# Thresholds from group maxima in the second attention step, with a list of rows done later

## The chip, the cores and the metric

The kernel runs on one core of a Trainium2 chip. The metric is the device time of one execution in microseconds (us); lower is better. Before the change the median of 3 runs was 5419.04 us (5407.9 to 5441.06). The engines are PE (TensorE, the matrix products; PEld are its weight loads), DVE (VectorE), ACT (ScalarE), POOL (GpSimd, which also issues DMAs) and SP (which issues DMAs).

## The reference, cut to what matters

Four graph layers over N = 4096 nodes with D = 256 features. Layers 0, 2 and 3 are products of the adjacency matrix with the features. Layer 1 makes two steps of attention in which each row keeps the largest probabilities until their sum reaches 0.9 of the whole ("top-p"):

```python
def _top_p_attention(X, W1, W2, W3):
    q = X @ W1.T @ W2.T
    k = X @ W3.T
    logits = q @ k.T / TAU
    probs = jax.nn.softmax(logits, axis=-1)
    idx = jnp.argsort(-probs, axis=-1)
    sp = jnp.take_along_axis(probs, idx, axis=-1)
    cs = jnp.cumsum(sp, axis=-1)
    keep_sorted = cs - sp < TOP_P
    ...
    A = probs * mask
    return A / jnp.maximum(A.sum(-1, keepdims=True), 1e-12)
...
for n in range(STEPS):
    A = _top_p_attention(Xa, W1, W2, W3)
    Xf = R @ Xf
    Xa = A @ Xa
    Z = Z + Xf @ U1[n].T + Xa @ U2[n].T
h = X + Z
```

Here n is step 0 and step 1, and R is the adjacency matrix with its diagonal raised by one, each row divided by its sum. The sort is stable, so among equal probabilities the node with the lower number comes first: where the threshold falls inside a set of equal ones, the first of them are kept and the last dropped. h is then normalized over its features, scaled and shifted, added to the layer's input and normalized once more.

## The kernel before, in words

The rows are worked in 32 tiles of 128 rows (P). For a tile the logits against all 4096 nodes form a 128 x 4096 array.

`run_step(n)` goes through i from -2 to 31 and holds three tiles at a time: nxt (tile i + 2), for which PE makes the logits, in 8 chunks of 512; cd (tile i + 1), for which DVE and ACT find the threshold; and st (tile i), for which `pieces` (L455) transposes the masked e on PE (`turn`, L468), copies it out on ACT (L470) and multiplies it with the features (acc_a, L487), beside the adjacency product (acc_r, L483; its blocks come over SP's queue, 256 KB each). `pieces` has 8 pieces, g = 0 to 7, and after piece g it issues what `ops` lists for g. `mix` (L504) then multiplies both results with U1 and U2 (z_ps, L515), and in step 0 makes the keys of step 1 (k_ps, L157). Within an engine the instructions run in a fixed order, which the framework sets when the kernel is built; it keeps nearly to the order of the program, and moves instructions forward when it reckons that they are ready.

Step 0 finds the threshold so: `peak_groups` (L287) takes the eight largest logits of each of 16 groups of 256 columns (MAX8, L277), 128 candidates; their maximum m goes to ACT, which makes e = exp(l - m) with its sum z (`exp_rows`, L279 to L285); `pick(cd, 6)` (L338) takes the 48 largest candidates in six rounds of MAX8 and match-replace, their running sum (L361), and the entry at which the sum reaches thr = 0.9 z (L366). A row is bad if the 48 don't reach so far or if a group's eighth candidate is not below the threshold. A one-column product on PE (bad_ps, L394) sums bad over the rows; `settle` (L404) reads the sum into a register of DVE (L411), branches on it, and then masks e in four quarters of 1024 columns, with their sums (L444). A tie at the threshold is told by v > 0, a row that isn't covered by v > P - 1.

Step 1 finds it in another way, whose cost lies on DVE: `peak` (L296) reduces the whole row for m; `bracket` (L301) makes five probes, each a pass over the 4096 columns that sums what is not below a trial value (L325), masks the array once more (L334) and takes MAX8 of 16 groups of it; `pick(cd, 8)` follows with 64 candidates; and `settle` always tells ties apart, with three passes: equality (L400), a running sum over the columns (L401), a difference (L402).

`bit_by_bit` (L416) is the way of last resort for a tile: 30 passes over the 4096 columns, each of which settles one bit of the threshold. It stands inside a branch.

The last layernorms of step 1 (`after`) run on DVE, with a power function on POOL (L147) in each. Layers 2 and 3 follow; layer 2 loads the result x2 in chunks (x2c, L626).

The thresholds' small arrays are [128, 1], the logits l and e are separate arrays with two buffers each.

Of the kernel before, what the change touches and what calls it, by code (L numbers as in the profile page):

```python
# [20 lines left out]
P = 128  # L21
D = 256
# [10 lines left out]
PROBES = 5  # L33
AIM = 0.65
# [5 lines left out]
def gnn_stack(ctx, tc, x, adjt, adjn, w0, b0, w1t, w2t, w3t, u1t, u2t, ln_g, ln_b, w2, b2, w3, b3, out):  # L40

# [37 lines left out]
    x2_d = dram.tile([N, D], F32, name="x2_d")  # L79
    x3_d = dram.tile([N, D], F32, name="x3_d")  # L80
    xa_d = dram.tile([N, D], F32, name="xa_d")
    h_d = dram.tile([N, D], F32, name="h_d")
# [150 lines left out]
    with tc.tile_pool(name="l1", bufs=1) as l1, tc.tile_pool(name="l1w", bufs=2) as l1w:  # L233
        g_sb = load_bcast(l1, ln_g, "g_sb")
        lb_sb = load_bcast(l1, ln_b, "lb_sb")
        cur = {}

# [6 lines left out]
        def query(n, i):  # L244

            lo, hi = DA * n, DA * (n + 1)
            xt = transposed(cur["xa"][:, i, :])
# [17 lines left out]
        def new_logits():  # L265
            return l1w.tile([P, N], F32, tag="l", name="l")

        def small(tag, w=1, dt=F32):
            return work.tile([P, w], dt, tag=tag, name=tag)
# [9 lines left out]
        def exp_rows(st):  # L279

            st["e"] = l1w.tile([P, N], F32, tag="e", name="e")
            st["z"] = z = small("z")
            nc.scalar.activation(st["e"], st["l"], AF.Exp, bias=st["m"], scale=1.0, accum_out=z)
            st["thr"] = small("thr")
            nc.vector.tensor_scalar(st["thr"], z, TOP_P, None, op0=ALU.mult)  # L285

        def peak_groups(st):  # L287

            st["cand"] = cand = small("cand", 8 * ngr)
            groups(st["l"], cand)  # L290
            st["m"] = m = small("m")
            nc.vector.tensor_reduce(m, cand, axis=AX.X, op=ALU.max)
            nc.vector.tensor_scalar(m, m, -1.0, None, op0=ALU.mult)
            st["base"] = None

        def peak(st):  # L296
            st["m"] = m = small("m")
            nc.vector.tensor_reduce(m, st["l"], axis=AX.X, op=ALU.max)
            nc.vector.tensor_scalar(m, m, -1.0, None, op0=ALU.mult)

        def bracket(st):  # L301


            e, thr = st["e"], st["thr"]
# [33 lines left out]
        def pick(st, rounds):  # L338

            cand, thr, base = st["cand"], st["thr"], st["base"]
            W = 8 * rounds
            g8 = small("g8")
            nc.vector.tensor_reduce(g8, cand.rearrange("p (g k) -> p g k", k=8)[:, :, 7], axis=AX.X, op=ALU.max)
            top = small("top", W)
# [6 lines left out]
            if base is None:  # L353
                nc.vector.memset(cs[:, 0:1], 0.0)
                te = small("te", W)
# [6 lines left out]
            last, part = small("last", W), small("part", W)  # L362
            nc.vector.tensor_scalar(part, cs[:, :W], thr, None, op0=ALU.is_lt)
            nc.vector.scalar_tensor_tensor(last, cs[:, 1:], thr, part, op0=ALU.is_ge, op1=ALU.mult)
            st["t"] = t = small("t_thr")
            nc.vector.scalar_tensor_tensor(part, last, 1.0, top, op0=ALU.mult, op1=ALU.mult, accum_out=t)  # L366
            bad = small("bad")
            nc.vector.tensor_tensor(bad, g8, top[:, W - 1 : W], op=ALU.max)
            nc.vector.tensor_tensor(bad, bad, t, op=ALU.is_ge)
            if base is None:  # L370
                nxt = small("nxt")
                nc.vector.scalar_tensor_tensor(part[:, 1:], last[:, : W - 1], 1.0, top[:, 1:], op0=ALU.mult, op1=ALU.mult,
                                               accum_out=nxt)
                nc.vector.tensor_tensor(nxt, nxt, t, op=ALU.is_ge)
                nc.vector.scalar_tensor_tensor(bad, bad, float(P), nxt, op0=ALU.mult, op1=ALU.add)
            else:
                nc.vector.tensor_scalar(bad, bad, float(P), None, op0=ALU.mult)  # L377

            def room():

                te_thr, r = small("t_e"), small("room")
                nc.vector.scalar_tensor_tensor(part, last, 1.0, te, op0=ALU.mult, op1=ALU.mult, accum_out=te_thr)
                nc.vector.scalar_tensor_tensor(part, te, te_thr, te, op0=ALU.is_gt, op1=ALU.mult, accum_out=r)
                nc.vector.tensor_add(r, r, cs[:, 0:1])
                nc.vector.tensor_sub(r, thr, r)
                tp = small("tp")
                nc.vector.tensor_scalar(tp, te_thr, 1e-30, None, op0=ALU.max)
                nc.vector.reciprocal(tp, tp)
                nc.vector.tensor_mul(r, r, tp)
                return te_thr, r  # L390

            st["room"] = room
            pb = ps_mm.tile([P, D], F32, tag="mm", name="bad_ps")
            nc.tensor.matmul(pb[:1, :1], bad, ones_col, start=True, stop=True)  # L394
            st["bad"] = pb

        def tell_apart(s, e, t, room):

            nc.vector.tensor_scalar(room, room, 1.0, TINY, op0=ALU.add, op1=ALU.mult)
            nc.vector.tensor_scalar(s, e, t, -TINY, op0=ALU.is_equal, op1=ALU.mult)  # L400
            nc.vector.tensor_tensor_scan(s, s, s, room, op0=ALU.add, op1=ALU.max)  # L401
            nc.vector.scalar_tensor_tensor(s, e, t, s, op0=ALU.subtract, op1=ALU.add)  # L402

        def settle(st):  # L404

            e, thr = st["e"], st["thr"]
            ties = st["base"] is not None
            nb = work.tile([1, 1], I32, tag="nbad", name="nbad")  # L410
            nc.vector.tensor_copy(nb, st["bad"][:1, :1])  # L411
            v = nc.vector.value_load(nb[0:1, 0:1])
            s = l1.tile([P, N], F32, tag="s", name="s")
            h, fl = small("mass"), small("flip", 1, I32)

            def bit_by_bit(t, room):  # L416
                ti = t.bitcast(I32)
                nc.vector.memset(ti, 1 << (ALL_BITS - 1))
                for b in range(ALL_BITS - 1, -1, -1):
                    nc.vector.scalar_tensor_tensor(s, e, t, e, op0=ALU.is_ge, op1=ALU.mult, accum_out=h)  # L420
                    nc.vector.tensor_scalar(fl, h, thr, float(1 << b), op0=ALU.is_lt, op1=ALU.mult)
                    nc.vector.scalar_tensor_tensor(ti, fl, (1 << b) >> 1, ti, op0=ALU.bitwise_or, op1=ALU.bitwise_xor)
                nc.vector.scalar_tensor_tensor(s, e, t, e, op0=ALU.is_gt, op1=ALU.mult, accum_out=h)
                nc.vector.tensor_sub(room, thr, h)
                nc.vector.reciprocal(h, t)
                nc.vector.tensor_mul(room, room, h)

            if ties:
                t, room = st["room"]()
                with tc.If(v > P - 1):  # L430
                    bit_by_bit(t, room)
                tell_apart(s, e, t, room)
            else:
                with tc.If(v > 0):
                    t, room = st["room"]()
                    with tc.If(v > P - 1):
                        bit_by_bit(t, room)
                    tell_apart(s, e, t, room)
                    nc.vector.scalar_tensor_tensor(e, s, 0.0, e, op0=ALU.is_ge, op1=ALU.mult)
                    nc.vector.memset(st["t"], -3e38)  # L440
            kq = small("kq", NQ)
            for c in range(NQ):
                q = slice(c * QW, (c + 1) * QW)
                nc.vector.scalar_tensor_tensor(e[:, q], (s if ties else st["l"])[:, q], 0.0 if ties else st["t"], e[:, q],  # L444
# [79 lines left out]
        def after(n, i, st):  # L524
# [8 lines left out]
            def s2():  # L533
                st["ln"] = ln_stats(st["h"])
# [189 lines left out]
```

## Time and profile before

| what | us |
|---|---|
| median of 3 runs | 5419.04 (5407.9 to 5441.06) |
| the profiled execution, its own time | 5451.28 |
| its span, first to last instruction | 5449.1 |
| busy PE / DVE / ACT / POOL in the span | 4525.2 / 3220.7 / 1143.6 / 518.0 |
| step 0: first logits to last product of acc_r | 718 to 2264 |
| step 1: first logits to last settle | 2284 to 4749 |
| layer 2's first product | 4783.5 |
| mean granted TensorE clock | 0.859 |

How to read it: the span is cut into 40 equal slices, and each digit is the busy share of an engine in tenths. A group line gives line, engine, operation, output<-input, shapes and count, then busy us and mean ns of one, then the engine's idle time just before these instructions and what ended it. A timeline line gives the start, the length, the instruction and, in brackets, the idle time before it. A matmul of 32-bit floats shows as two instructions.

### The profile page before, as it was taken

The page shows a single profiled execution, that of the slowest core. Times are in us where ns is not written, and L with a number is a line of the kernel's source. Part 1 is how long each engine was busy: PE and PEld are TensorE (multiplying, and loading weights), DVE is VectorE, ACT ScalarE, POOL GpSimd, SP SyncE. Part 2 cuts the span into 40 slices and gives each one's busy share as a digit, 9 for nine tenths or more (in the row PEclk, how much of TensorE's full clock was granted, in tenths as well). Part 3 has the DMA queues.
Part 4 walks back from the last instruction along what each step waited for, and adds up shares of the span by engine and source line. Part 5 has one row for each costly group of instructions (what it writes and reads, how often), then busy time and mean ns, then how long its engine had stood idle before and what let it go on. Part 6 is the DMA issues. An engine that isn't in the chain of part 4 may idle for free. (4 is left out here: it accounts for less than half of the span.)

```text
span 5449.1 us, 54173 instructions
## 1 busy us (share of the span) xinstructions
PE 4525.2 (83%) x19520; PEld 3347.0 (61%) x19520; DVE 3220.7 (59%) x7924; ACT 1143.6 (21%) x1969; POOL 518.0 (10%) x966
## 2 busy tenths in 40 slices
PE   9999999999999899946766777666766767489999
PEld 7888866666666666735544555445544555467776
DVE  1111143333333433199999999999999999833322
ACT  1000033333333323212211222121221212011100
POOL 4444300000000000000000000000000000022222
PEclk8998799999999999867777777777777777799999
DMA  8777621111111111201101110111101111077787
GB/s 225 220 213 206 176 62 50 51 50 49 50 51 49 44 50 49 87 22 37 30 27 36 37 37 24 33 36 37 37 21 35 37 37 30 21 226 225 228 247 223
DMA packets 246758, 464.20 MB, mean 85 GB/s; under 512 B 26643, under 2 KB 82582, under 8 KB 246422
## 3 DMA queue, kind: packets, MB, share of 16 engines
q0 software_dynamic: 110592, 268.48, 17.2%
q1 hardware_dynamic: 128192, 184.60, 11.2%
q10 hardware_dynamic: 7638, 7.10, 0.4%
q8 instruction: 154, 2.52, 0.2%
q14 instruction: 182, 1.49, 0.1%
HBM read 434.92 MB, written 25.17 MB: 84 GB/s over the span
## 5 line engine op out<-in xcount | busy, mean ns | idle before, releaser
L262 PE MATMUL lg<-kT,qT 64*128 64x512 f32 x1024 | 732.6, 852 | 10.4 <-ACT qT L256 10.4
L325 DVE SCALAR_TENSOR_TENSOR junk<-e,pr 128x4096 f32<-128x4096 f32 x160 | 716.4, 4477 | 3.5
L277 DVE MAX8 cand<-l 128x8 f32<-128x256 f32 x512 | 194.5, 418 | 727.5 <-ACT l L263 727.0
L483 PE MATMUL acc_r<-x,adjq 128*128 128x256 f32 x2048 | 502.6, 386 | 59.7 <-ACT xa_new L495 57.7
L468 PE MATMUL at_ps<-ident,e 128*128 128x128 f32 x2048 | 346.3, 300 | 243.3 <-DVE e L444 243.3
L487 PE MATMUL acc_a<-xa,at 128*128 128x256 f32 x2048 | 530.8, 406 | 0.0
L468 PEld LDWEIGHTS at_ps<-ident,e 128*128 128x128 f32 x2048 | 259.5, 153 | 434.9 <-issue 417.5
L263 ACT COPY l<-lg 128x512 f32<-128x512 f32 x512 | 299.5, 585 | 1046.8 <-PE lg L262 1046.2
L487 PE MATMUL acc_a<-x,at 128*128 128x256 f32 x2048 | 488.4, 381 | 0.0
L147 POOL TENSOR_TENSOR rstd<-ve,mhalf 128x1 f32<-128x1 f32 x160 | 89.2, 558 | 4062.9 <-DVE ve L145 3847.6
L394 PE MATMUL bad_ps<-ones_col,bad 128*1 128x1 f32 x128 | 12.1, 164 | 537.3 <-DVE bad L377 537.3
L483 PE MATMUL acc_r<-xf_next,adjq 128*128 128x256 f32 x2048 | 452.7, 381 | 0.1
L483 PEld LDWEIGHTS acc_r<-x,adjq 128*128 128x128 f32 x2048 | 367.3, 191 | 135.4 <-ACT xa_new L495 65.0
L262 PEld LDWEIGHTS lg<-kT,qT 64*128 64x128 f32 x1024 | 236.2, 253 | 333.3 <-issue 200.4
L470 ACT COPY at<-at_ps 128x512 f32<-128x512 f32 x512 | 299.9, 586 | 664.7 <-PE at_ps L468 655.4
L487 PEld LDWEIGHTS acc_a<-xa,at 128*128 128x128 f32 x2048 | 400.9, 205 | 60.5 <-ACT at L470 8.8
L487 PEld LDWEIGHTS acc_a<-x,at 128*128 128x128 f32 x2048 | 387.6, 190 | 74.4 <-issue 22.7
L483 PEld LDWEIGHTS acc_r<-xf_next,adjq 128*128 128x128 f32 x2048 | 388.5, 191 | 54.9 <-issue 2.8
L123 PE MATMUL acc<-x0h,adjt 128*128 128x512 f32 x1024 | 345.9, 460 | 9.0 <-DMA adjt<-in_adjt 7.1
L394 PEld LDWEIGHTS bad_ps<-ones_col,bad 128*1 128x1 f32 x128 | 5.5, 81 | 561.2 <-DVE bad L377 550.2
L107 POOL DMA_DIRECT2D adjt<-in_adjt x512 | 279.3, 545 | 509.5 <-PE acc L123 400.2
L401 DVE TENSOR_TENSOR_SCAN s<-s,room 128x4096 f32<-128x4096 f32 x33 | 288.8, 8751 | 1.2
(184 smaller groups left out, 6230.1 us busy)
## 6 DMA issues: line engine op xcount, KB each, us to landing
adjq<-in_adjt SPq DMA_DIRECT2D x512, 256.0 KB, 2.8
adjt<-in_adjt POOLq DMA_DIRECT2D x256, 512.0 KB, 5.1
adjt<-in_adjt POOLq DMA_DIRECT2D x256, 256.0 KB, 4.3
adjn<-in_adjn POOLq DMA_DIRECT2D x256, 256.0 KB, 4.1
x_d<-x SPq DMA_DIRECT2D x64, 128.0 KB, 3.8
x<-in_x ACTq DMA_DIRECT2D x4, 1024.0 KB, 10.2
x1r<-x_d SPq DMA_DIRECT2D x32, 128.0 KB, 2.0
xa_d<-xa_new SPq DMA_DIRECT2D x32, 128.0 KB, 1.7
```

What stands on the lines that cost most here:

```text
L107: (nc.gpsimd if dt is F32R else nc.sync).dma_start(t, src[it, :, c * jp : (c + 1) * jp, :])
L123: nc.tensor.matmul(acc, a[:, j, :], halves(jt), start=(jt == 0), stop=(jt == NT - 1))
L147: nc.gpsimd.tensor_tensor(r, ve, mhalf, op=ALU.pow)
L262: nc.tensor.matmul(pl[:, :LC], qT, kT[DA * n : DA * (n + 1), s], start=True, stop=True)
L263: nc.scalar.copy(l[:, s], pl[:, :LC])
L277: nc.vector.max(dst[:, 8 * g : 8 * g + 8], src[:, g * GW : (g + 1) * GW])
L325: nc.vector.scalar_tensor_tensor(junk, e, pr[:, 0:1].bitcast(F32), e, op0=ALU.is_ge, op1=ALU.mult, accum_out=mass[id(pr)])
L401: nc.vector.tensor_tensor_scan(s, s, s, room, op0=ALU.add, op1=ALU.max)
L468: nc.tensor.transpose(ps[:, j, :], e[:, (g * G + j) * P : (g * G + j + 1) * P], ident)
L470: nc.scalar.copy(ats[g][:, :G, :], ps[:, :G, :])
L483: nc.tensor.matmul(acc_r[:, :D], adjs[g][:, j, :], cur["xf"][:, jt, :], start=(jt == 0), stop=False)
L487: nc.tensor.matmul(acc_a[:, :D], ats[g][:, j, :], cur["xa"][:, jt, :], start=(jt == 0), stop=(jt == NT - 1))
```

## The change

Step 1 now uses the way of step 0 for its 32 tiles, with eight rounds. Rows that this doesn't settle are listed in memory (their numbers, by a scatter from POOL), up to LATER * P = 512 of them; after the 32 tiles four more tiles are run, whose rows are gathered by that list and which use the bracket. A tile whose unsettled rows would not fit into the list runs `bit_by_bit` in place. The masks of both steps no longer tell ties apart with passes: pick counts `left`, how many entries equal to the threshold have to be dropped, and one match-replace over the row (with eight pad columns of -1) sets the first `left` of them to 0; the host reverses the nodes, so that the first in the array are the last in the reference. A row with left above PAD = 8 counts as bad. In step 0 and in the four tiles, any bad row sends the whole tile through `bit_by_bit`. e is computed in place of l, in three buffers.

In the diff, cut to its core, "..." marks what is left out.

```diff
+LATER = 4
+PAD = 8
...
+    x2_d = dram.tile([N + LATER * P, D], F32, name="x2_d")
...
+    xf_d = dram.tile([N, D], F32, name="xf_d")
+    list_d = dram.tile([(LATER + 1) * P, 1], I32, name="list_d")
...
         def new_logits():
-            return l1w.tile([P, N], F32, tag="l", name="l")
+            l = l1w.tile([P, N + PAD], F32, tag="e", name="e", bufs=3)
+            nc.vector.memset(l[:, N:], -1.0)
+            return l
...
         def exp_rows(st):
-            st["e"] = l1w.tile([P, N], F32, tag="e", name="e")
+            e = st["e"][:, :N]
             st["z"] = z = small("z")
-            nc.scalar.activation(st["e"], st["l"], AF.Exp, bias=st["m"], scale=1.0, accum_out=z)
+            nc.scalar.activation(e, e, AF.Exp, bias=st["m"], scale=1.0, accum_out=z)
...
-            last, part = small("last", W), small("part", W)
-            nc.vector.tensor_scalar(part, cs[:, :W], thr, None, op0=ALU.is_lt)
-            nc.vector.scalar_tensor_tensor(last, cs[:, 1:], thr, part, op0=ALU.is_ge, op1=ALU.mult)
+            under, part = small("under", W), small("part", W)
+            count = small("count")
+            nc.vector.tensor_scalar(under, cs[:, :W], thr, 0.0, op0=ALU.is_lt, op1=ALU.add, accum_out=count)
+            nc.vector.scalar_tensor_tensor(part, cs[:, 1:], thr, under, op0=ALU.is_ge, op1=ALU.mult)
             st["t"] = t = small("t_thr")
-            nc.vector.scalar_tensor_tensor(part, last, 1.0, top, op0=ALU.mult, op1=ALU.mult, accum_out=t)
-            bad = small("bad")
-            nc.vector.tensor_tensor(bad, g8, top[:, W - 1 : W], op=ALU.max)
+            nc.vector.scalar_tensor_tensor(part, part, 1.0, te[:, :W], op0=ALU.mult, op1=ALU.mult, accum_out=t)
+            st["left"] = left = small("left")
+            nc.vector.tensor_scalar(part, te[:, :W], t, 0.0, op0=ALU.is_ge, op1=ALU.add, accum_out=left)
+            nc.vector.tensor_sub(left, left, count)
+            st["bad"] = bad = small("bad")
+            nc.vector.tensor_tensor(bad, te[:, W - 1 : W], te[:, W:], op=ALU.max)
             nc.vector.tensor_tensor(bad, bad, t, op=ALU.is_ge)
...
+            nc.vector.scalar_tensor_tensor(bad, left, float(PAD), bad, op0=ALU.is_gt, op1=ALU.max)
+
+        def flag(st):
+            pb = ps_mm.tile([P, D], F32, tag="mm", name="bad_ps")
+            if st.get("later") is None:
+                nc.tensor.matmul(pb[:1, 0:1], st["bad"], ones_col, start=True, stop=True)
             else:
...
+                nc.tensor.matmul(pb[:, 0:1], ones_sq, st["bad"], start=True, stop=True)
+                nc.tensor.matmul(pb[:, 1:2], before, st["bad"], start=True, stop=True)
+            st["bad_ps"] = pb
+
+        def bit_by_bit(st, s):
+            e, thr, t = st["e"][:, :N], st["thr"], st["t"]
+            h, fl, room = small("mass"), small("flip", 1, I32), small("room")
+            ti = t.bitcast(I32)
+            nc.vector.memset(ti, 1 << (ALL_BITS - 1))
+            for b in range(ALL_BITS - 1, -1, -1):
+                nc.vector.scalar_tensor_tensor(s, e, t, e, op0=ALU.is_ge, op1=ALU.mult, accum_out=h)
+                nc.vector.tensor_scalar(fl, h, thr, float(1 << b), op0=ALU.is_lt, op1=ALU.mult)
+                nc.vector.scalar_tensor_tensor(ti, fl, (1 << b) >> 1, ti, op0=ALU.bitwise_or, op1=ALU.bitwise_xor)
+            nc.vector.scalar_tensor_tensor(s, e, t, e, op0=ALU.is_gt, op1=ALU.mult, accum_out=h)
+            nc.vector.tensor_sub(room, h, thr)
+            nc.vector.reciprocal(h, t)
+            nc.vector.tensor_mul(room, room, h)
+            nc.vector.tensor_scalar(s, e, t, 0.0, op0=ALU.is_equal, op1=ALU.add, accum_out=h)
+            nc.vector.tensor_add(room, room, h)
+            nc.vector.tensor_scalar(room, room, -TINY, None, op0=ALU.mult)
+            nc.vector.tensor_scalar(s, s, TINY, None, op0=ALU.mult)
+            nc.vector.tensor_tensor_scan(s, s, ones_col.to_broadcast([P, N]), room, op0=ALU.add, op1=ALU.min)
             nc.vector.scalar_tensor_tensor(s, e, t, s, op0=ALU.subtract, op1=ALU.add)
+            nc.vector.scalar_tensor_tensor(e, s, 0.0, e, op0=ALU.is_gt, op1=ALU.mult)
+            nc.vector.memset(t, 1e-37)
+            nc.vector.memset(st["left"], 0.0)

         def settle(st):
...
+            if later is None:
+                nc.vector.tensor_copy(nb, pb[:1, :1])
+            else:
+                sofar = small("sofar")
+                nc.vector.tensor_add(sofar, later["base"], pb[:, 0:1])
+                nc.vector.tensor_scalar(nb, sofar[:1, :1], float(LATER * P), None, op0=ALU.is_gt)
+                slot = small("slot")
+                nc.vector.tensor_add(slot, later["base"], pb[:, 1:2])
             v = nc.vector.value_load(nb[0:1, 0:1])
             s = l1.tile([P, N], F32, tag="s", name="s")
...
+            with tc.If(v > 0):
+                bit_by_bit(st, s)
+                if later is not None:
+                    nc.vector.memset(st["bad"], 0.0)
+                    nc.vector.tensor_copy(sofar, later["base"])
+            if later is not None:
+                it = later["tile"]
+                at = small("at", 1, I32)
+                nc.vector.tensor_sub(slot, slot, spare)
+                nc.vector.scalar_tensor_tensor(at, slot, st["bad"], spare, op0=ALU.mult, op1=ALU.add)
+                later["base"] = sofar
+                nc.gpsimd.indirect_dma_start(
+                    out=list_d, out_offset=bass.IndirectOffsetOnAxis(ap=at[:, 0:1], axis=0),
+                    in_=ids[:, it : it + 1], in_offset=None)
+            go, no, eight = small("go", PAD), small("no", PAD), small("eight", PAD)
+            nc.vector.tensor_scalar(go, count8, left, None, op0=ALU.is_lt)
+            nc.vector.tensor_scalar(no, go, -1.0, None, op0=ALU.add)
+            nc.vector.scalar_tensor_tensor(eight, go, t, no, op0=ALU.mult, op1=ALU.add)
+            nc.vector.match_replace(e, eight, e, 0.0)
             kq = small("kq", NQ)
             for c in range(NQ):
                 q = slice(c * QW, (c + 1) * QW)
-                nc.vector.scalar_tensor_tensor(e[:, q], (s if ties else st["l"])[:, q], 0.0 if ties else st["t"], e[:, q],
-                                               op0=ALU.is_ge, op1=ALU.mult, accum_out=kq[:, c : c + 1])
+                nc.vector.scalar_tensor_tensor(e[:, q], e[:, q], t, e[:, q], op0=ALU.is_ge, op1=ALU.mult,
+                                               accum_out=kq[:, c : c + 1])
...
+        def gathered(src, st, tag):
+            t = work.tile([P, D], F32, tag=tag, name=tag)
+            nc.gpsimd.indirect_dma_start(
+                out=t, out_offset=None, in_=src, in_offset=bass.IndirectOffsetOnAxis(ap=st["from"][:, 0:1], axis=0))
+            return t
...
+        def put_off(k):
+            st = {"tile": None}
+            st["to"] = to = small("to", 1, I32, LATER)
+            nc.sync.dma_start(to, list_d[k * P : (k + 1) * P, :])
+            st["from"] = fr = small("from", 1, I32, LATER)
+            nc.vector.tensor_scalar(fr, to, float(N - 1), None, op0=ALU.min)
+            st["q"] = query(n, gathered(xa_d, st, "xg"))
+            st["e"] = new_logits()
+            return st
...
+            end = NT + 1 + LATER if last_step else NT
+            for i in range(-2, end):
...
+                elif NT < i + 2 < end:
+                    nxt = put_off(i + 2 - NT - 1)
...
+                if cd is not None and cd["tile"] is not None:
+                    if later is not None:
+                        later["tile"] = cd["tile"]
+                    peak_groups(cd)
+                    at(1, exp_rows, cd)
+                    at(2, pick, cd, 8 if last_step else 6)
+                    at(4, flag, cd)
+                    at(5, settle, cd)
+                    pieces(n, st, nxt, ops)
                 else:
                     if cd is not None:
                         bracket(cd)
...
+                    pieces(n, st, nxt, ops)
                     if cd is not None:
                         pick(cd, 8)
+                        flag(cd)
+                if nxt is not None and nxt["tile"] is None:
+                    peak(nxt)
+                    exp_rows(nxt)
+                if cd is not None and cd["tile"] is None:
+                    settle(cd)
...
+    x = np.asarray(x)[::-1]
+    adj = np.asarray(adj)[::-1, ::-1]
...
+    return r.results[0]["out"][::-1]
```

Before the change `pick` and `settle` stood at pieces 3 and 4 in step 0. In the four added tiles `pieces` makes no acc_r: xf is stored to xf_d by the 32 tiles of step 1 and gathered, as are h_d, x1_d and xa_d, and the result is scattered to x2_d.

## The prediction

> **What bounds the kernel now.** I read the slices first, then the windows (busy time of each engine in a stretch), the waits of step 1, the groups by cost and shape, and the timelines of one tile.
>
> ```profile
> PE   9999999999999899946766777666766767489999
> DVE  1111143333333433199999999999999999833322
> PEclk8998799999999999867777777777777777799999
> ```
> Each digit is one slice of 136 us. In slices 5 to 16 (step 0) TensorE is full and VectorE works a third of the time. In slices 17 to 34 (step 1) it is the other way round.
>
> ```profile
> 1400.00:1800.00 400.00, 385.22 (x1707) 273.84 (x1707) 143.81 (x525) 135.59 (x229) 0.00 (x0) 1.00 0.16 50
> 3000.00:4000.00 1000.00, 698.95 (x2678) 503.72 (x2678) 959.46 (x2045) 204.68 (x330) 14.24 (x26) 0.74 0.11 33
> ```
> Columns: window, length, then busy us of PE, PEld, DVE, ACT, POOL, the granted clock, DMA. Step 0 has PE at 96%; step 1 has DVE at 96% and PE at a clock of 0.74, because it waits:
>
> ```profile
> PE bad_ps L394 <- DVE bad L377: 475.9, 30, 16.5
> PE at_ps L468 <- DVE e L444: 214.5, 30, 21.1
> ```
> (us in total, times, longest.) The DVE work of a step-1 tile is full-width passes:
>
> ```profile
> L325 DVE SCALAR_TENSOR_TENSOR junk<-e,pr 128x4096 f32<-128x4096 f32 x160 | 716.4, 4477 | 3.5
> L401 DVE TENSOR_TENSOR_SCAN s<-s,room 128x4096 f32<-128x4096 f32 x33 | 288.8, 8751 | 1.2
> L402 DVE SCALAR_TENSOR_TENSOR s<-e,t_e,s 128x4096 f32<-128x4096 f32 x33 | 148.0, 4485 | 1.2
> L334 DVE SCALAR_TENSOR_TENSOR junk<-e,hi 128x4096 f32<-128x4096 f32 x32 | 143.5, 4484 | 0.1
> L298 DVE TENSOR_REDUCE m<-l 128x1 f32<-128x4096 f32 x32 | 141.2, 4414 | 80.6 <-ACT l L263 80.6
> L400 DVE TENSOR_SCALAR s<-e,t_e 128x4096 f32<-128x4096 f32 x33 | 77.4, 2345 | 0.0
> ```
> No row of bit_by_bit (L420 to L426) exists: that branch never ran. L401 ran 33 times, once in step 0. The period of a tile is 76.2 us in step 1 (first L325 of two tiles, 2999.42 and 3075.64) and 48.19 in step 0 (the two lines of PE's wait below, 48.20 apart):
>
> ```profile
> 1646.27 1.13 PE L483 MATMUL acc_r<-x,adjq 128*128 128x256 f32 x4 [1.64 <-ACT xa_new L495]
> 1694.47 1.13 PE L483 MATMUL acc_r<-x,adjq 128*128 128x256 f32 x4 [1.65 <-ACT xa_new L495]
> ```
> That 1.65 us is all that PE idles in a step-0 tile.
>
> **Ordinary tiles of step 1.** They lose the bracket and the tie passes. What stays on DVE: 16 MAX8 of 0.42 (6.7 us), pick with eight rounds (8 x 0.29 + 7 x 0.37 = 4.9, and 2.5 of small operations), the layernorm (4), match-replace over 4104 elements, four quarters of 1.22 (4.9), some 20 small operations of 0.15 (3). Match-replace has only a row at 128 elements, 0.276; MAX8 takes 0.293 there and 0.418 at 256, so 1 ns an element more, which makes 4.2 to 4.4; the bounds are 2.3 (L400, the fastest full pass) and 8.75 (the scan), I take 4.4. Sum about 30 us. PE then paces, as in step 0.
>
> Does DVE stay in time? In step 0 bad is ready at 1649.5, bad_ps runs at 1671.56 in its place after a piece, the last quarter ends 1677.9, and PE's next transposes start at 1692.2: 14.3 us to spare. The change moves flag one piece later (5.1 us) and adds match-replace (4.4) and three small operations (0.5): 4.3 us are left. The layernorm waits for h (1662.3) and is done near 1668, in front of bad_ps at 1676.7. But the MAX8 of the last chunks now queue behind settle: six of them after 1688, so the maximum comes about 1.2 us later than 1690.0, and exp on ACT with it. ACT's copy of xa_new stands behind that exp, and PE waits for it (the 1.65). If the order is kept PE idles 1.2 to 1.5 more; if xa_new goes in front, 0.6 less. I take +0.6 for each tile of both steps. Step 1 saves k_ps (0.58) and has two flag products instead of one (0.2): 48.19 + 0.6 - 0.4 = 48.4.
>
> The list scatter (512 bytes) and the xf_d store (128 KB) lie on POOL and SP; POOL's next pow comes some 20 us after the scatter, and the DMA share of step 1 is 0.11. Behind the scatter's wait for slot only that pow is queued, whom DVE waits for. Cost nothing, covered by those 20 us; uncovered it would be about the 2.0 us in which a 128 KB load lands, per tile.
>
> **Step 0.** 29 full tiles at +0.6: +17. The tile with a tie (L400, L401, L402, L439 from 1866.9 to 1887) goes through match-replace instead. Tiles 1 to 30 ended at 2228.74 from 775.93, 1452.8 against 29 x 48.19 + 35.0 = 1432.5: so -20. Sum -3.
>
> **The four put-off tiles.** Here I counted rows, by carrying out the reference's arithmetic on its inputs: 426 rows of 4096 are not settled by groups (513 would overflow the list), so four tiles of 128, 128, 128 and 42 rows. But in step 0 many rows keep one neighbour alone; rows with the same one get equal xa, thus equal keys and exactly equal logits, in sets of up to 19. 37 rows have more than PAD = 8 ties to drop, and 11, 15, 10 and 1 of them fall into the four tiles. Such a row sets bad in pick whatever the bracket found (the set's place in the row and the sizes of the shares leave the count of ten in the fourth tile a margin of over one per cent of the mass); settle then has v > 0 and runs bit_by_bit over the whole tile. The kernel before told ties apart with one scan of any length and never came there.
>
> Price of one loop: a pass to the next dependent operation is 4.53 (2331.32 to 2335.85), and two dependent operations at 0.19: 4.91, thirty times 147.4. Behind it a pass (4.5), three small ones (0.6), a pass that counts equals (2.35 by L400 to 4.48 by L325, whose form also sums; I take 4.4), 0.4, a scaling pass 2.35, the scan 8.75, two passes of 4.49, 0.1: 30.1. Together 177.5 us.
>
> The rest of such a tile on DVE: five probes 31.1 (6.22 each, 2325.10 to 2331.32), L334 4.5, MAX8 5.3, pick 7.5, flag and branch 1.9 (3049.0 to 3050.9), next tile's maximum 4.4, match-replace and its values 4.9, quarters 4.8, layernorm 1.6 beyond gaps: 66.0. Sum 243.5; four of them 974, less 6 for the last, which has no next maximum, and the first, which has no layernorm: 968. All of it is one chain: each tile's bracket waits on DVE for the settle before it. PE's 30 us for such a tile and the gathers lie beside it.
>
> **The sum.** Before: first logits of step 1 at 2283.9, first matmul of layer 2 at 4783.5: 2499.6. After: to the end of tile 0, as in step 0 (718.05 to 775.93) 57.9, and 14 for the slow clock at the start (16 logits matmuls took 14.02 there, 0.53 each at full rate would be 8.4, and the query with them): 72. 29 x 48.4 = 1403.6. Tile 30 without logits 35.0 (2228.74 to 2263.76), tile 31 with those of the first put-off tile 45. Its maximum and exp 9.5 (4.4 + 3.9 and small ones). Tail 968. From the last settle to layer 2 34.5 (4749.0 to 4783.5). Gathers and the last scatter lie on the path only at the end: loads and stores of that size land in 1.7 to 4.4 us, two in a row 3.4 to 8.8, I take 6. Sum 2573.6, which is +74. With step 0: +71.
>
> The profiled execution took 5451.3 (span 5449.1), so it would take 5522. It lies 32 above the median of 5419: predicted 5490.
>
> One rule against a row. After 3 us of waiting at 2274.7 PE's rate was half for some 40 us; after 21 us at 4673 it recovered within 5 (eight acc_a 2.73, then 1.89). The Trainium skill, TensorE: Matmul & The Clock Gate, Part 1, says that about 3.4 us of sustained work release the clock; by it the 14 us would be an estimated 2, and the sum 12 lower. Another speaks against the change: Runtime: NRT & Kernel Launch, Instruction fetch mechanics, says a taken branch out of the fetched window stalls for a DMA. The trace has 0.5 to 1.1 us after a branch, and 3.4 at most at L399; it would be up to 14 in four tiles, which I leave to the range.
>
> **Rivals.**
> - Loops not run (chances 0.05 and 0.06). Ties are equal only if equal rows stay equal in every bit; a fully dropped row adds zeros, which speaks for it. The fourth tile hangs on one row (ten ties): without it 5490 - 178 = 5312. Without any: 5490 - 710 = 4780. The sign turns when three loops or fewer run.
> - DVE sets the pace of ordinary tiles (0.07): the layernorm's two trips to POOL before pick, settle past 1692. The 4.3 us left speak against it. At 3 us a tile more, +90: 5580.
> - The list overflows (0.01): each tile past 512 runs a loop in place, 178 each. 426 rows are 86 short.
>
> **How the numbers follow.** Four loops has 0.81. Its own bounds: the idle term -0.6 to +1.5 over 58 tiles (-70, +52), step 0's tie tile (+20), equals pass (-8), match-replace in the tail (-8, +17), branches (+14), ends (-3, +15), start (-12, if it recovers as after the 21 us): they don't all fall together, and I take 5400 to 5600. With part of the stall case and for the spread of the runs (5408 to 5441), 8 in 10 lie in 5400 to 5620. About 1% (54 us) is what a measurement of this kernel can tell from no change. Within four loops 0.68 lie above 5473 and 0.31 within: slower 0.55 + 0.08 = 0.63, same 0.25, faster 0.12.
>
> **What would show it.** The profile after should have about 124 new 128x4096 passes in bit_by_bit, four scans, a period of 48.4 in the first 32 tiles of step 1 with the clock at 1.0, then some 970 us of full DVE with PE near idle. Fewer than four scans, or a period above 50, proves a step wrong.

## The result and the profile after

The changed kernel takes 5670.23 us (median of 4 runs, 5667.59 to 5726.44) against 5430.05 of the kernel before in the same comparison (5407.9 to 5442.82). The ratio is 1.0481, interval 1.0419 to 1.0543: slower, as forecast, but by 240 us instead of the 71 forecast, and above the range (5400 to 5620). The profiled execution is the slowest of its kernel, 5726.44 us; 29 us of that lie ahead of the end of step 0's first tile, nearly all of it in layer 0, which the change does not touch (the first xa_new of step 0 is copied at 807.8 us, before it was at 778.3).

The slices of the changed kernel, 143 us each:

```profile
PE   9999999999999999999999999999402101079999
DVE  1111153443344434265555554554799999933322
PEclk9989799999999999899999999999655555589999
```

Step 1 no longer has VectorE at its limit (digits 4 to 6 where 9s stood), TensorE is full up to slice 28, and then comes a stretch of seven slices in which VectorE is nearly full (7, then 9s) and TensorE nearly idle: the four put-off tiles. In the windows (length, then busy us of PE, PEld, DVE, ACT, POOL with the instructions, granted clock, DMA share, GB/s) the first is step 0, the second the ordinary tiles of step 1, the third the tail:

```profile
1400.00:1800.00 400.00, 380.31 (x1614) 267.78 (x1613) 172.76 (x540) 125.38 (x212) 0.00 (x0) 0.95 0.16 47
3000.00:3900.00 900.00, 846.98 (x3584) 605.51 (x3584) 473.79 (x1556) 274.97 (x452) 38.01 (x53) 0.95 0.23 52
4045.00:5016.00 971.00, 114.64 (x410) 76.61 (x411) 942.89 (x1128) 46.01 (x73) 18.03 (x17) 0.54 0.01 2
```

TensorE's waits of the whole execution (us in total, times, longest) answer to those that led its list before, where 32 waits for bad came to 537 us and 33 for e to 243. Now four tiles wait for their loop, and 59 for a copy:

```profile
PE at_ps L508 <- DVE e L481: 726.1, 4, 190.8
PE acc_r L524 <- ACT xa_new L537: 172.8, 59, 5.0
```

The tail is the forecast one: 971.3 us from the start of the first bracket (4045.1) to the end of the last settle (5016.4), forecast 968. New groups of VectorE, by cost and shape, carry it: 120 passes are four loops of thirty, all in the tail, so no ordinary tile ran a loop and the list did not overflow. Of the 68 match-replaces four lie there.

```profile
L422 DVE SCALAR_TENSOR_TENSOR s<-e,t_thr 128x4096 f32<-128x4096 f32 x120 | 538.1, 4485 | 4.2
L477 DVE MATCH_REPLACE8 e<-eight,e 128x4104 f32<-128x4104 f32 x68 | 300.4, 4418 | 0.0
L435 DVE TENSOR_TENSOR_SCAN s<-s,room,ones_col 128x4096 f32<-128x4096 f32 x4 | 35.0, 8752 | 0.1
```

The surprise is in the windows' clock: 0.95 where step 0 had 1.00 before. A tile of step 0 took 48.2 us; now the periods, from one copy of xa_new to the next, go 49.0, 53.8, 49.0, 53.8 and so on, 52.0 in the mean, and 51.2 in step 1. TensorE's timeline of two tiles that follow each other (start, duration, instruction, in brackets the idle time before it and who ended it):

```profile
1540.56 1.13 PE L524 MATMUL acc_r<-x,adjq 128*128 128x256 f32 x4 [2.47 <-ACT xa_new L537]
1544.23 2.07 PE L524 MATMUL acc_r<-x,adjq 128*128 128x256 f32 x4
1548.24 3.78 PE L528 MATMUL acc_a<-x,at 128*128 128x256 f32 x8
1594.33 1.13 PE L524 MATMUL acc_r<-x,adjq 128*128 128x256 f32 x4 [2.44 <-ACT xa_new L537]
1599.03 1.99 PE L528 MATMUL acc_a<-x,at 128*128 128x256 f32 x8
```

Both tiles wait 2.4 to 2.5 us for ScalarE's copy, 0.8 more than before. In the first, four instructions that take 1.13 take 2.07 a little later, and eight take 3.78; in the second eight take 1.99. The windows of the first tile give the reason:

```profile
1541.00:1546.00 5.00, 5.00 (x18) 3.05 (x16) 1.75 (x14) 1.96 (x6) 0.00 (x0) 0.57 0.07 26
1546.00:1552.00 6.00, 6.00 (x12) 3.07 (x11) 0.75 (x2) 0.59 (x1) 0.00 (x0) 0.50 0.15 44
1552.00:1558.00 6.00, 6.00 (x28) 4.39 (x28) 0.76 (x2) 1.58 (x3) 0.00 (x0) 1.00 0.15 44
```

TensorE is busy without a break, but the granted clock falls to one half for 10.2 us and comes back. The tile is 4.8 us longer for it, six times as much as the wait grew. Such tiles (over 52 us) are 16 of 29 in step 0 and 12 of 29 in step 1.

Where the wait comes from is read on VectorE's timeline of the same tile:

```profile
1524.18 4.42 DVE L477 MATCH_REPLACE8 e<-eight,e 128x4104 f32<-128x4104 f32 x1
1533.66 0.08 DVE L481 DVE_READ_ACCUMULATOR e<-e,t_thr 128x1 f32 x1
1534.85 0.73 DVE L304 MAX8 cand<-e 128x8 f32<-128x256 f32 x2
1536.11 0.13 DVE L320 TENSOR_SCALAR m<-m 128x1 f32<-128x1 f32 x1
```

Settling ends at 1533.7; the MAX8 that stood behind it come after that, the maximum at 1536.2, and on ScalarE the exponential and then the copy:

```profile
1536.34 3.71 ACT L310 ACTIVATE e<-e,m 128x4096 f32<-128x4096 f32 x1 [2.36 <-DVE m L320]
1540.05 0.46 ACT L537 ACTIVATE xa_new<-acc_a,sc 128x256 f32<-128x256 f32 x1
```

Theory: the longer wait, which comes from the later settling, lets the clock drop; the wait is paid in all 58 tiles and the clock in about half of them. Rivals: the wait alone costs (then its removal gives some 50 us); or the slow tiles come from what VectorE or the transfers do beside TensorE, whatever the wait is; and for the size of the whole, that the loops cost other than forecast.

### The profile page after: what moved, and what is told of

Read it like the earlier page. It is cut to its first block, busy times and chain, and to the rows that moved or that the text cites. A ratio compares the mean times of both kernels' runs of the same rounds, so it can differ in the third digit from the quotient of the medians.

```text
span 5724.7 us, 54976 instructions
## 1 busy us (share of the span) xinstructions
PE 4612.2 (81%) x20128; PEld 3388.9 (59%) x20128; DVE 2818.3 (49%) x7151; ACT 1214.5 (21%) x2097; POOL 584.2 (10%) x1031
## 5 line engine op out<-in xcount | busy, mean ns | idle before, releaser
L304 DVE MAX8 cand<-e 128x8 f32<-128x256 f32 x1024 | 393.8, 417 | 1174.6 <-ACT e L287 1174.1
L287 ACT COPY e<-lg 128x512 f32<-128x512 f32 x544 | 318.8, 586 | 1585.6 <-PE lg L286 1585.6
L286 PE MATMUL lg<-kT,qT 64*128 64x512 f32 x1088 | 648.9, 687 | 0.7 <-ACT qT L280 0.7
L524 PE MATMUL acc_r<-xf_next,adjq 128*128 128x256 f32 x2048 | 520.3, 395 | 90.1 <-ACT xa_new L537 90.0
L422 DVE SCALAR_TENSOR_TENSOR s<-e,t_thr 128x4096 f32<-128x4096 f32 x120 | 538.1, 4485 | 4.2
L481 DVE SCALAR_TENSOR_TENSOR e<-e,t_thr 128x1024 f32<-128x1024 f32 x272 | 332.4, 1278 | 0.1
L141 ACT COPY xt<-tr 128x256 f32<-128x256 f32 (+1 forms) x264 | 125.8, 478 | 854.7 <-PE tr L139 845.1
L477 DVE MATCH_REPLACE8 e<-eight,e 128x4104 f32<-128x4104 f32 x68 | 300.4, 4418 | 0.0
L286 PEld LDWEIGHTS lg<-kT,qT 64*128 64x128 f32 x1088 | 177.0, 200 | 191.0 <-issue 161.3
L310 ACT ACTIVATE e<-e,m 128x4096 f32<-128x4096 f32 x68 | 252.3, 3710 | 175.1 <-DVE m L320 168.8
```

The costliest lines, as they stand in the source:

```text
L286: nc.tensor.matmul(pl[:, :LC], qT, kT[DA * n : DA * (n + 1), s], start=True, stop=True)
L287: nc.scalar.copy(l[:, s], pl[:, :LC])
L304: nc.vector.max(dst[:, 8 * g : 8 * g + 8], src[:, g * GW : (g + 1) * GW])
L477: nc.vector.match_replace(e, eight, e, 0.0)
L481: nc.vector.scalar_tensor_tensor(e[:, q], e[:, q], t, e[:, q], op0=ALU.is_ge, op1=ALU.mult, accum_out=kq[:, c : c + 1])
L524: nc.tensor.matmul(acc_r[:, :D], adjs[g][:, j, :], cur["xf"][:, jt, :], start=(jt == 0), stop=False)
```

## The experiments

**The flag and the settling one piece earlier**, where the kernel before had them.

```diff
-                    at(4, flag, cd)
-                    at(5, settle, cd)
+                    at(3, flag, cd)
+                    at(4, settle, cd)
```

> flag and settle go back to pieces 3 and 4, nothing else. Theory (clock gate): in the changed kernel settle ends late, the last MAX8 queue behind it, the maximum and exp come 0.8 us later, PE's gap at the start of a tile grows from 1.65 to 2.45 us, and after such a gap PE runs at half rate for some microseconds in about every second tile (periods of 49.0 and 53.8). Then this edit brings the gap back to 1.65 and all periods to about 48: 29 x (52.0 - 48.2) + 29 x (51.2 - 47.9) = some 205 less than the changed kernel's 5670, so about 5465. Rival (the longer gap alone, without a slow clock after it): 58 x 0.8 = 46 less, 5624. Rival (match-replace or the shared buffers slow the tiles, wherever settle stands): 5670, no change.

Measured: 5469.92 us, ratio to before 1.0075 (1.0032 to 1.0118). Every ordinary tile of step 0 but the first takes 48.2, and every one of step 1 but the first 47.7. TensorE's waits in 1000 to 1800 us (in total, times, longest) are those of the kernel before to the digit, and the clock is back:

```profile
PE acc_r L524 <- ACT xa_new L537: 27.9, 17, 1.6
```

```profile
1000.00:1800.00 800.00, 772.07 (x3420) 549.59 (x3419) 357.71 (x1132) 266.25 (x451) 0.00 (x0) 1.00 0.17 50
```

So 200 us of the 240 come from where the flag stands, and not from the four loops being dearer than forecast. What is left, 40 us or 0.75%, is the change proper: fewer passes in step 1, against 970 us of tail.

**TensorE kept busy in the wait**: five products that nobody reads, before the transposes of each ordinary tile. The settling stays late.

```diff
                 st = tiles.pop(i, None)
+                if st is not None and st["tile"] is not None:
+                    fill = ps_mm.tile([P, D], F32, tag="mm", name="fill_ps")
+                    for _ in range(5):
+                        nc.tensor.matmul(fill, ident, cur["xf"][:, 0, :], start=True, stop=True)
```

> The order of the changed kernel is kept; five products of PE with no use (2.2 us) stand at the start of each ordinary tile, ahead of its transposes, in the gap. Theory (clock gate): the gap that is left is about 0.4 us, PE never slows down, every period is about 49.0: 29 x 3.0 + 29 x 2.3 = some 155 less than 5670, about 5515, though PE has 126 us more to do. Rival (the late exp itself, or anything on DVE, makes the 53.8): 5670. Rival (PE is simply full): about 125 more, 5795.

Measured: 5588.5 us, ratio 1.0255 (1.02 to 1.031): about half of the expected gain. Most tiles now take 49.0 and 48.8, the time of the fast tiles of the kernel after, at clock 1.00. The copy is not earlier, and TensorE's timeline shows the fill and what is left of the wait in one tile, and a tile where it fails:

```profile
1037.67 2.32 PE L634 MATMUL fill_ps<-x,ident 128*128 128x256 f32 x10
1040.95 1.13 PE L524 MATMUL acc_r<-x,adjq 128*128 128x256 f32 x4 [0.31 <-ACT xa_new L537]
1337.42 1.48 PE L524 MATMUL acc_r<-x,adjq 128*128 128x256 f32 x4 [2.74 <-ACT xa_new L537]
```

The work that fills a wait buys the clock, not the wait: the five products cost what they replace. In the last line TensorE waited 2.4 us longer still. VectorE's timeline of that tile has the likely reason, and the second line here is an ordinary tile:

```profile
1320.24 0.23 DVE L474 TENSOR_SCALAR go<-count,left 128x8 f32<-128x8 f32 x1 [3.52 <-DVEq L457]
1023.76 0.23 DVE L474 TENSOR_SCALAR go<-count,left 128x8 f32<-128x8 f32 x1 [1.07 <-DVEq L457]
```

The branch around the loop, taken past it, costs 1.07 us, but 3.5 in a few tiles. Where settling has time to spare this is hidden (in the run above the same branches wait 39.5 us in the 32 tiles of step 0, and only the first tile is longer); here it is not. In the kernel after, three of the four long waits of step 0 and all five of step 1 (4.8 to 5.0 us) also stand behind a branch of 3.3 to 3.6. By the profiles the 58 tiles gained 112 us of the expected 155, and tiles in which the fill fails are what is missing there; the rest of the missing half stays open.

**Two and three match-replaces in the put-off tiles**, so that 16 or 24 ties can be dropped before the loop is needed. The count of ties is held against PAD times the rounds, and settle repeats its last lines (here with three; 2 stands for 3 in the other kernel):

```diff
-            nc.vector.scalar_tensor_tensor(bad, left, float(PAD), bad, op0=ALU.is_gt, op1=ALU.max)
+            st["drops"] = 3 if base is not None else 1
+            nc.vector.scalar_tensor_tensor(bad, left, float(PAD * st["drops"]), bad, op0=ALU.is_gt, op1=ALU.max)
...
-            nc.vector.tensor_scalar(go, count8, left, None, op0=ALU.is_lt)
+            for d in range(st["drops"]):
+                if d:
+                    nc.vector.tensor_scalar(left, left, -float(PAD), None, op0=ALU.add)
+                    nc.vector.memset(e[:, N:], -1.0)
+                nc.vector.tensor_scalar(go, count8, left, None, op0=ALU.is_lt)
...
-            nc.vector.match_replace(e, eight, e, 0.0)
+                nc.vector.match_replace(e, eight, e, 0.0)
```

> In the four put-off tiles alone, two match-replaces in a row, so that up to 16 ties can be dropped before a row counts as bad. By the count of rows only two rows (18 ties to drop each, both in the third put-off tile) stay above that: one loop instead of four. Theory: 5670 - 3 x 177.5 + 4 x 5 = about 5158. Rival (bad rows in these tiles come from the bracket, not from ties): all four loops stay, about 5690. Rival (the tail is slow for another reason than the loop): less than 100 gained.

> As the one with two, with three match-replaces in the put-off tiles (up to 24 ties; the largest count is 18): no loop at all. Theory: 5670 - 4 x 177.5 + 4 x 10 = about 5000, and no instruction of the loop in the profile. Rivals as before: about 5710, or some of the loops left, 177 each.

Measured: 5182.01 us with two (ratio 0.9496, 0.9435 to 0.9557) and 5015.53 with three (0.9205, 0.9154 to 0.9257). The groups count the loops: with two drops one is left, with three no line of the loop exists and only the match-replace has grown. First the kernel with two, then with three:

```profile
L423 DVE SCALAR_TENSOR_TENSOR s<-e,t_thr 128x4096 f32<-128x4096 f32 x30 | 134.5, 4484 | 1.0
L482 DVE MATCH_REPLACE8 e<-eight,e 128x4104 f32<-128x4104 f32 x72 | 318.1, 4418 | 0.0
```

```profile
L482 DVE MATCH_REPLACE8 e<-eight,e 128x4104 f32<-128x4104 f32 x76 | 335.8, 4418 | 0.0
```

All four loops gone give 655 us. The eight further match-replaces cost about 42 (5.3 each with their small operations), so a loop is worth (655 + 42) / 4 = 174 us; the forecast had 177.5. The price of the loops stands, and the rival that makes them the cause of the miss falls.

**Both at once**: the earlier flag and three drops.

> The flag of step 1 at piece 3 and the settling at piece 4, and three match-replaces in the put-off tiles, so that both changes of the earlier runs are made at once. The theory (two costs that have nothing to do with each other: the half clock behind the gap of the tensor engine, and the loops of the tail) adds the gains: 5670 less 200 (the earlier flag) less 655 (three drops) = 4815. A theory in which the gain of the earlier flag is partly the run-to-run state of the chip gives some 4900. Periods of an ordinary tile 48.2 in step 0 and 47.7 in step 1, no instruction of the loop.

Measured: 4785.0 us, ratio 0.8823 (0.8759 to 0.8887). The two gains add, to within 0.6% (4815 expected): the cost of the clock and that of the loops do not depend on each other.

**The exponential in two halves**, the settling late as in the kernel after. The copy that TensorE waits for runs between them.

```diff
-            nc.scalar.activation(e, e, AF.Exp, bias=st["m"], scale=1.0, accum_out=z)
+            zz = small("zz", 2)
+            for c in range(2):
+                half = e[:, c * N // 2 : (c + 1) * N // 2]
+                nc.scalar.activation(half, half, AF.Exp, bias=st["m"], scale=1.0, accum_out=zz[:, c : c + 1])
+            nc.vector.tensor_add(z, zz[:, 0:1], zz[:, 1:2])
```

> The kernel after the change with one edit: the exponential of a tile in two halves of 2048 instead of one of 4096, and the two sums added. ScalarE then does the copy that the tensor engine waits for between the halves. The flag and the settling stay where they are, so the maximum comes as late as in the kernel after. Theory (the clock halves behind a wait of 2.45 us, and the wait is set by the end of the whole exponential): the wait falls by the second half, some 1.9 us, to 0.6 us, the clock stays at its height, the periods are about 47.2 in step 0 and 46.8 in step 1, and the time is 5670 less 59 tiles of about 4.5 = 5400. If the slow stretches came from the vector engine's settling or from the transfers beside it, and not from the wait, the periods stay at 51 to 52 less the 1.9 of the wait at most: 5560.

Measured: 5432.86 us, ratio 1.004 (1.0001 to 1.0079). Most periods are 47.2 and 47.0, at clock 1.00, though the maximum comes as late as in the kernel after. ScalarE's timeline of a tile, and TensorE's wait in it:

```profile
1102.90 2.01 ACT L313 ACTIVATE e<-e,m 128x2048 f32<-128x2048 f32 x1 [2.30 <-DVE m L324]
1104.90 0.45 ACT L541 ACTIVATE xa_new<-acc_a,sc 128x256 f32<-128x256 f32 x1
1106.34 2.03 ACT L313 ACTIVATE e<-e,m 128x2048 f32<-128x2048 f32 x1
```

```profile
1105.41 1.13 PE L528 MATMUL acc_r<-x,adjq 128*128 128x256 f32 x4 [0.70 <-ACT xa_new L541]
```

So the wait, and not the settling beside it, makes the slow tiles: the settling was not moved here, and they are gone. About one tile in four still takes 48.6 to 50.2, some of them where the branch takes 3.3 to 3.6 us.

**All three together**: earlier flag, three drops, halves.

> Earlier flag, three match-replaces and the exponential in halves together. The theory: with the flag earlier the wait is 1.6 us, and the halves take some 1.3 of it away in 59 tiles, so about 4815 less 60 = 4755, with periods of 47.0 and 46.6. If ScalarE's later half delays the copies of the next products instead, 4815 or a little more.

Measured: 4676.09 us, ratio 0.8605 (0.8542 to 0.8667), the fastest version found. The gain is larger than expected, since no wait is left at all. In the windows TensorE is busy for 800.00 of 800 and 1000.00 of 1000 us, and the periods are 46.4 and 45.9:

```profile
1000.00:1800.00 800.00, 800.00 (x3555) 569.37 (x3553) 372.18 (x1176) 276.12 (x498) 0.00 (x0) 1.00 0.18 52
2300.00:3300.00 1000.00, 1000.00 (x4446) 724.03 (x4444) 589.32 (x1956) 345.79 (x607) 47.11 (x66) 1.00 0.27 58
```

**The wait by itself, in three doses.** The flag is early, so settling is out of the way; the 0.29 us reduction that ends the maximum is done two, four or seven times (the diff is that of the first dose).

```diff
-            nc.vector.tensor_reduce(m, cand, axis=AX.X, op=ALU.max)
+            for _ in range(2):
+                nc.vector.tensor_reduce(m, cand, axis=AX.X, op=ALU.max)
```

> The earlier flag and settling (5470 us, wait of the tensor engine 1.6 us, periods 48.2 and 47.7), and the 0.29 us reduction that makes the maximum done twice, so that the exponential and the wait come 0.29 us later: a wait of 1.9 us. Nothing else on the vector engine moves. If the clock's limit lies above that, the periods grow by the 0.3 alone (48.5 and 48.0) and the time is 5470 and 59 tiles of 0.29 = 5487. If the limit lies between 1.6 and 1.9, some tiles take 53 and the time is up to 5650. A theory in which the half clock of the kernel after comes from the settling beside the start of a tile, not from the wait's length, gives 5487 too.

> The same with the reduction done four times: the maximum 0.87 us later and the wait 2.5 us, as in the kernel after, with the settling out of the way. If the length of the wait alone makes the half clock, about every second tile takes 53 to 54 again and the time is that of the kernel after, some 5660. If the settling beside the tile's start makes it, the clock stays at its height, the periods are 49.1 and 48.6, and the time is 5470 and 59 times 0.87 = 5521.

> The same with the reduction done seven times: the maximum 1.74 us later and the wait 3.4 us. If the half clock comes the more often the longer the wait is, all or nearly all of the 59 tiles have it, at 4.8 each: periods of about 54.7 and 54.3, and 5470 and 59 times 6.5 = 5855. If its share stays at a half, 5470 + 59 x (1.74 + 2.4) = 5715. Without any effect of the clock 5573.

Measured: 5541.47 us (ratio 1.0255, 1.0166 to 1.0343), 5676.09 (1.0466, 1.0369 to 1.0563) and 5339.35 (0.988, 0.9793 to 0.9967).

The second is the kernel after again, without its late settling: the same slow tiles, the same time. With e6 this closes the question from both sides. The doses in a table, of step 0 alone (slow: over 52 us; in step 1 the first dose has only 3 of 29):

| kernel | wait, us | fast tile | slow tile | slow of |
|---|---|---|---|---|
| before, earlier flag | 1.64 | 48.2 | 53.0, 53.8 | only the tile behind a wait of 3.7 or 10.3 |
| reduction twice | 1.96 | 48.5 | 53.3 | 10 of 29 |
| after | 2.45 | 49.0 | 53.8 | 16 of 29 |
| reduction four times | 2.60 | 49.2 | 53.9 | 16 of 29 |

The first dose in TensorE's timeline: the same wait in both tiles, the clock down in one of them.

```profile
991.96 1.13 PE L525 MATMUL acc_r<-x,adjq 128*128 128x256 f32 x4 [1.96 <-ACT xa_new L538]
999.42 3.78 PE L529 MATMUL acc_a<-x,at 128*128 128x256 f32 x8
1045.25 1.13 PE L525 MATMUL acc_r<-x,adjq 128*128 128x256 f32 x4 [1.97 <-ACT xa_new L538]
1049.95 1.99 PE L529 MATMUL acc_a<-x,at 128*128 128x256 f32 x8
```

The traces tell which tiles it is. They hold the moments at which the granted clock changed, and in each trace all of these lie on one grid of 3.413 us (55 changes with the first dose, each within 0.01 us of it). The first dose has 57 waits of 1.96 us in both steps: the clock fell behind all 13 that ended 1.83 us or more after a line of the grid, and behind none of the 44 that ended 1.77 or less after one. The regular waits of the kernel after, 2.44 to 2.74 us, part at the same place, 25 against 24. Of the waits of 1.64 with the earlier flag 27 of 56 end as late, and the clock falls behind none. The half clock lasts three steps of the grid, 10.2 us, and one step, 3.4 us, where a regular wait of the kernel after ended 2.73 or more after a line; such a tile is some 1.5 us longer.

The third dose was no dose, and all my expectations for it failed. Making the maximum later still changed the order in which ScalarE gets its work:

```profile
1020.68 0.47 ACT L538 ACTIVATE xa_new<-acc_a,sc 128x256 f32<-128x256 f32 x1 [3.07 <-PE acc_a L529]
1021.08 3.71 ACT L310 ACTIVATE e<-e,m 128x4096 f32<-128x4096 f32 x1
```

The copy now stands in front of the exponential, waits only for the product it copies, and TensorE has no wait: periods of 46.3 and 45.8, and 1.2% less than the kernel before with all four loops still in the tail. What I had put at 3.4 us of waiting became 0. The order of the queues comes out of the build, which moved the copy by itself in this dose; by what rule it does so was not tried.

## Why the prediction failed, point by point

**The step that failed is the idle term of ordinary tiles**, "I take +0.6 for each tile of both steps", with bounds of -0.6 and +1.5. The chain was right link by link: the MAX8 stand behind the settling (maximum 1.2 us later forecast, the wait 0.8 longer in the trace), the exponential and the copy follow, and TensorE's wait grows from 1.65 to 2.45. Two things were wrong in its price. Between the ends (order kept, 1.2 to 1.5; copy in front, -0.6) I took a value in the middle, though the two are orders of one queue and only one can be: the order was kept. And I priced a wait of TensorE at its own length. The clock behind it costs six times the growth of the wait, in about half the tiles. Measured in step 0 52.0 - 48.2 = +3.8 a tile: some 1.1 is the wait, four waits of 4.3 to 5.0 us included, and 2.7 the clock. In step 1, where a tile with the early flag takes 47.7 (predicted without the term 47.8), 51.2 - 47.7 = +3.5.

The clue stood in the profile of before: behind the tie tile TensorE waited 10.3 us, and the tile that began so took 53.8 instead of 48.2, with the clock at 0.50 (a line of TensorE's timeline, then one of the windows):

```profile
1899.88 2.07 PE L483 MATMUL acc_r<-x,adjq 128*128 128x256 f32 x4 [10.29 <-ACT xa_new L495]
1900.00:1911.00 11.00, 11.00 (x26) 6.40 (x27) 2.41 (x12) 2.86 (x8) 0.00 (x0) 0.50 0.12 37
```

I took what both tiles had over as "-20" for the tie and did not ask why the second was longer, so my upper bound left the clock out.

**What this leaves of the sum.** Without the term, 58 x 0.6 less, the forecast is 5455; the kernel with the earlier flag took 5470. By parts of the profiled execution, step 0 came at +93 against -3, the 29 ordinary tiles of step 1 at 1485.3 against 1403.6. The rest held: start of step 1 62.3 (72), tile 30 34.1 (35), tile 31 52.5 (45), tail 971.3 (968), from the last settle to layer 2 42.6 (40.5). Add 29 for layer 0, and the 204 us between 5726 and the 5522 forecast are accounted for to within 5.

**The put-off tiles** were right: four loops, one for each tile, the fourth too; 243.7, 242.9 and 235.2 us from one to the next against 243.5; match-replace 4.418 us against 4.4; the pass that counts equals 4.48 against 4.4. Loops not run falls as a rival, though its price was right: three drops show what the kernel is without them, 655 us less, where I had put 710.

**Step 0's tie tile** was right: with the early flag no tile of step 0 but the first differs, and the 18 us that it and its successor cost before (60.8 + 53.8 - 2 x 48.2) are gone.

**DVE sets the pace** is not what happened. VectorE was busy for 53% of the window of step 1 that is shown above; it was late at one place, by 0.8 us in step 0.

**The weighed rules.** On the clock I set a rule against a row only for the start of step 1. There the row was the nearer one for the clock itself, 0.52 over 25 us (2405 to 2430) in which TensorE was busy throughout. But it cost less than I had made of the row: the start took 62.3 us, where the row gave 72 and the rule an estimated 60.

For the waits, the Trainium skill, TensorE: Matmul & The Clock Gate, Part 1, says that an idle window of about 3.4 us halves the clock and that this window is free-running and does not start anew with the kernel. The traces agree that the place of a wait in time matters, by their grid of 3.413 us: with one and the same wait of 1.96 us some tiles are slow and some are not, in step 0 mostly every third (three tiles of the first dose take 150.3 us, an estimated 44.0 windows of the page's 3.413 us). They differ in the length: 1.96 us of idling, 2.6 counted from the last product over the transposes, are enough in 10 of 29 tiles of step 0. Isolated waits in the kernel with halves fit the grid too: two of 2.63 and 3.03 us ended 1.77 and 1.60 after a line and left the clock alone, two of 2.83 and 2.93 ended 3.3 after one, and their tiles were 1.6 us longer. Why the half clock lasts three steps in some tiles and one in others was not tried.

On the branch, the row held where it was used (no sign of the 14 us in the tail, 971.3 against 968). But I had looked at the branch only in the put-off tiles. The skipped one in each ordinary tile costs 1.07 us and at times 3.5, and with the settling later it had lost its cover; whether code loading makes the difference was not tried.

## What to carry to other kernels

Price a wait of TensorE that recurs in every tile by the clock behind it: here 1.64 us was free of it and 1.96 cost 4.8 us in a third of the tiles of step 0. When a change makes an engine later ahead of such a wait, look in the trace of before for a tile that waited longer once, and read its length and the next one's. And if the copy that ends the wait stands behind long work in its queue, splitting that work or moving the copy in front of it is worth more than the lateness itself: in both versions the tiles of step 0 ran faster than in the kernel before (47.2 and 46.3 against 48.2).

## What was not expected of the hardware

- The granted clock fell to 0.50, mostly for 10.2 us, behind waits of 1.96 to 2.74 us that ended 1.8 us or more after a line of a 3.413 us grid, never behind regular ones of 1.64; a tile then takes 4.8 us more.
- A branch that skips the loop held VectorE for 1.07 us in most tiles and mostly 3.3 to 3.8 in a few.
- A TENSOR_SCALAR that also sums took 4.48 us over 4096 elements (L431), one without a sum 2.35 in the trace of before (L400).
- The indirect DMA that writes the list occupied GpSimd for 1.03 us a tile, off the path.
